# Two attention layers over patches: who reads layer 1's logits back, and when a patch's reads, jobs and first rows are issued

## The chip, the cores and the metric

The kernel runs on one core of one Trainium2 chip. TensorE (PE in the profile) multiplies matrices, VectorE (DVE), ScalarE (ACT) and GpSimd (POOL) do elementwise work, and SyncE (SP) only issues transfers (DMAs). ScalarE and GpSimd issue DMAs too. Each issuing engine has its own DMA queue: the profile calls SyncE's q1, GpSimd's q0 and ScalarE's q10. Every engine takes its instructions in order, and an instruction that waits holds up all behind it on that engine.

The metric is device time in microseconds, as the median of several runs. Before the change it is 3497.4 us (three runs, 3495.59 to 3503.78).

## What is computed

The input is x, 8 images of 56 x 56 pixels with 384 channels, all in float32. Both layers normalise x in 32 groups of channels, apply an attention over each pixel's 3 x 3 neighbourhood, and add the result to x:

```
layer 0 (12 heads): v = xn Wv;  a = softmax(xn Wa / sqrt(32)), 9 x 9 weights per pixel and head
                    out[p] = sum_q a[p,q] v[neighbour q];  y = out folded back onto the neighbours;  x += y Wo
layer 1 (6 heads):  v = xn W_v + b_v;  a = softmax(xn W_attn + b_attn), 9 weights per pixel and head
                    y = sum_k a[k] v[neighbour k];  x += y W_proj + b_proj
```

## The kernel before

**Tiling.** Two images make a pair (NPAIR = 4), and a pair's column of 2 x 56 = 112 pixels is the unit of work. Layer 0 walks over the 4 x 56 columns, one column a *step*; the step number divided by 56 gives pair and column c. Of eight columns only seven are worked on by themselves: a TensorE tile has 128 rows, so the eighth column's pixels (c % 8 == 7) ride along in the 16 spare rows of the other seven, and that step has no attention of its own. Seven columns make a *patch* (PX = 7, eight patches a pair).

**Layer 0, one step.** `attend` does three logit matmul groups (tile `bank`, from `wa_t`), with VectorE taking maximum and difference of each, ScalarE the exponential, and one matmul group for v. Between these groups `between(n)`, n = 0 to 3, slips in the work of earlier columns: for n = 0 the transposes of the next pair's rows (`turned`, `stats_chunk`, tile `pt` from `xr`), the normalising of the column before (`normalise`, then `presum` on GpSimd, tile `pre`) and one job; for n = 1 the matmul `pw` of `fold` (the column three back); for n = 2 another job; for n = 3 the rest, and one more job in a step with c % 8 == 7. `fold` ends in two writes of the column's weights to the table `ztab` in DRAM, and `keep_v` stores v to `vtab` through GpSimd. `share_out` moves the eighth column's pieces over the scratch tensor `last` or directly (`at`).

**Layer 0, one patch.** When a patch's columns are all in the tables, `fetch_v` (line 765) reads v of both images (vp, 1536 KB each) and one step later `fetch` (line 782) reads the weights of both (z, 2352 KB each; one z tile per image, two vp tiles). `fetch` also queues the patch's ten jobs, all due four steps later: four `contract` jobs (tile `pc`, copied to `yT`) and six `project_out` jobs (tile `po`, added to `xres` as `x1t`). `Jobs.run(step, n)` runs the first n jobs whose due step has come, in the order in which they were queued, so ten jobs run two a step in five steps. `held_back` (line 929) keeps jobs out of two steps near the end.

**Before and around the steps.** At the start (lines 512 to 525) the rows of pair 0 are loaded in 14 blocks, transposed, and copied to DRAM by `keep_block`; then `clear_first` writes zeros into the tables. The rows of the next pair are loaded block by block with `stats_load`, one every three steps, from `upkeep` (line 866), the first one at c = 0, and used three steps later. `upkeep` also clears z at step 8 (lines 874 to 876) and issues the clearing of further tables, six writes each, at steps that `clears` gives. All of these loads, copies, clears, table writes and patch reads are issued by SyncE, in program order.

**Layer 1** works on groups of seven columns (g, 32 of them, m = 0 to 6 within a group), from 2246 us on. `attend` makes logits (tile `lgt`) and v together. When a group is done its logits are written to DRAM by ScalarE (`keep_logits`, table `lgtab`), read back with one pixel row a partition by `read_logits` (line 1073, tile `at`), and then go through `weigh` (maximum and exponential), `share` (sum, reciprocal, product) and `move` (a shift matmul `pw` on TensorE, copies into `wz`, a write to `ztab1`). A group later `fetch` (line 1133) reads z and vp for its contraction:

```
            done, last = g - 1, g == NG
            read, first, second, moved = (0, 2, 3, 4) if last else (1, 3, 4, 5)
...
            if m == 1 and g + 1 < NG:
                load(g + 1)
            if g > 1 and m == 0:
...
                fetch(done - 1, base + step + 3)
            if g and m == read:
                read_logits(done)
```

`weigh` runs at m = 3, `share` at 4, `move` at 5. In layer 1 SyncE's calls are held in program order (`sync` is `InOrder`, line 134 of the profile is its helper); the v stores and the output stores go through `nc.gpsimd` directly, and are placed by the builder.

Of the kernel before, what the change touches and what calls it, by code (L numbers as in the profile page):

```python
# [8 lines left out]
F32 = mybir.dt.float32  # L9
# [6 lines left out]
def two_outlook_layers(  # L16
# [77 lines left out]
    EP1, FIRST1 = 11, 4  # L94
    SLOT0, SLOT1 = EP0 * ROW0, EP1 * ROW1
    LINE0, LINE1 = SX0 * SLOT0 + ROW0, SX1 * SLOT1 + ROW1
    NTAB = 2

    xf = x.rearrange("b y x c -> (b y) x c")
    of = out.rearrange("b y x c -> (b y) x c")  # L100
# [5 lines left out]


    vtab0 = dram.tile([NPX * (R + GAP) + GAP, SX0, C], F32, name="vtab0")
    ztab0 = [dram.tile([RT + 1, LINE0], F32, name=f"ztab0_{n}") for n in range(NTAB)]
    vtab1 = dram.tile([NPX * (R + GAP) + GAP, SX1, C], F32, name="vtab1")  # L110
    ztab1 = [dram.tile([RT + 1, LINE1], F32, name=f"ztab1_{n}") for n in range(NTAB)]
    lgtab = dram.tile([NPAIR * W * R, NA1], F32, name="lgtab")
    xTs = [dram.tile([P, NCH, W * R], F32, name=f"xT_{pair}") for pair in range(NPAIR)]
    x1s = [dram.tile([NPX, P, NCH, T], F32, name=f"x1_{pair}") for pair in range(NPAIR)]
# [306 lines left out]
    def layer0(late, pools):  # L421
# [93 lines left out]
        for blk in range(NBLK):  # L515
# [4 lines left out]
                    pass  # L520
            if blk == 1:
                wv_t = weight(fixed, wv0, C, "wv0_t", sync)
        for blk in (1, 4, 0, 2, 3, *range(5, NBLK)):
            keep_block(0, blk)
        clear_first()
        warm = stat.tile([P, 1], F32, tag="warm", name="warm", bufs=1)
# [195 lines left out]
        def fold(pair, c):  # L722

            pre = pres.pop((pair, c)).rearrange("r (pi qi) f h -> r pi qi f h", qi=K)
            parts = []
            for px, sx in patches_of(c, 2):
                wt, to, f0, f1 = weights_of(sx)
                for e, pi, qi in ((0, 0, 2), (E0 - 1, 2, 0)):  # L730
                    scalar.activation(
                        to[:, e], pre[:, pi, qi, f0:f1, :], AF.Copy, scale=inside[:R, 0, qi : qi + 1]
                    )
                parts.append((px, sx, wt, to, f0, f1))
            pw = ps.tile([R, E0, E0, HEADS0], F32, tag="f", name=f"pw_{pair}_{c}")
            for qi in (0, 2):
                lo = qi // 2
                matmul(
                    pw[:, 2 - qi + lo : 4 - qi + lo], shift[:, qi, :], pre[:, lo : lo + 2, qi],
                    start=(qi == 0), stop=(qi == 2), skip_group_check=True,  # L740
                )
            for px, sx, wt, to, f0, f1 in parts:
                vector.tensor_tensor(
                    to[:, 1 : 1 + K], pw[:, 1 : 1 + K, f0:f1, :], pre[:, :, 1, f0:f1, :], ALU.add
                )
            yield
            for px, sx, wt, to, f0, f1 in parts:
                at = sx * SLOT0 + FIRST0 * ROW0
                table = ztab0[(pair * NPX + px) % NTAB]
                first = table.offset + MARGIN * LINE0 + at  # L750
                weights = wt.rearrange("r e h m -> r e (h m)")
                sync.dma_start(
                    bass.AP(table.tensor, first + ROW0, [[LINE0, R], [1, K * ROW0]]),
                    weights[:, 1 : 1 + K].rearrange("r e a -> r (e a)"),
                )
                sync.dma_start(
                    bass.AP(
                        table.tensor, first + LINE0,
                        [[LINE0, R], [(E0 - 1) * ROW0 - 2 * LINE0, 2], [1, ROW0]],
                    ),  # L760
                    weights[:, 0 : E0 : E0 - 1],
                )
            yield

        def fetch_v(pair, px):

            vps[:] = [patch_tiles(f"0_{pair}_{px}", b) for b in range(IMG)]
            for b in range(IMG):
                rows_to_patches(sync, vps[b], vtab0, px, b * H, PY0, NPY0, SX0)

        vps = []

        xres = {}

# [4 lines left out]
                lambda: sync.dma_start(xres[pair, px], xTs[pair][:, :, px * T : (px + 1) * T])  # L779
            )  # L780

        def fetch(pair, px, due, final=None):

            nm = f"0_{pair}_{px}"
            n_tile = 2
            yT = projected(nm)
            if not pair and not px:
                load_res(0, 0)
            for b in range(IMG):
                z, vp = zs[b], vps[b]  # L790
                bands(
                    sync, z, ztab0[(pair * NPX + px) % NTAB], LINE0, SLOT0, ROW0, 0, GROUPS0,
                    b, PY0, NPY0,
                )

                def contract(t, b=b, z=z, vp=vp):
                    pc = ps.tile([P, NCH, n_tile, PY0, PX], F32, tag="c", name=f"pc_{nm}_{b}_{t}", bufs=NC)
                    for n in range(n_tile):
                        py = t * n_tile + n
                        zp = z[: SX0 * SY0, py].rearrange("s (y h m) -> s y h m", y=PY0, h=HEADS0)  # L800
                        for h in range(HEADS0):
                            i, j = divmod(h, P // D0)
                            matmul(
                                pc[j * D0 : (j + 1) * D0, i, n],
                                vp[: SX0 * SY0, py, h * D0 : (h + 1) * D0],
                                zp[:, :, h, :],
                                start=True, stop=True,
                            )
                    rows_of = slice(t * n_tile * PY0, (t + 1) * n_tile * PY0)
                    scalar.copy(  # L810
                        yT[:, :, :, b, rows_of], pc.rearrange("p i n y m -> p i m (n y)")
                    )

                for t in range(0, NPY0 // n_tile, NC):
                    jobs.add(due, lambda t=t, f=contract: [f(t + n) for n in range(NC)])
            if pair == NPAIR - 1 and px == NPX - 1:
                jobs.add(due, clear_bands)
            if px == 0:
                st1s[pair] = stat.tile([P, NCH, IMG, 2 * NPX, 6], F32, tag="st1", name=f"st1_{pair}")

            def project_out(half, j):
# [2 lines left out]
                po = ps.tile([P, 4 * R], F32, tag="o", name=f"po_{nm}_{half}_{j}")  # L824
                project_half(po, wo_t, yT, half, j)
                if j == 0:
                    fetch.x1t = late_w.tile([P, NCH, 4, R], F32, tag="x1t", name=f"x1t_{nm}_{half}", bufs=2)
                x1t = fetch.x1t
                vector.tensor_tensor(
                    x1t[:, j].rearrange("p m r -> p (m r)")[:, :n], po[:, :n],  # L830
                    xres[pair, px][:, j, lo * R : hi * R], ALU.add,
# [16 lines left out]
                        if following[0] < NPAIR:  # L848
                            load_res(*following)

            for half in range(2):
                for j in range(NCH):
                    jobs.add(due if final is None else final, lambda half=half, j=j: project_out(half, j))
            if px == NPX - 1:
                def params_part(n):
                    if n == 0:
                        making["1"] = norm_params(st1s.pop(pair), f"1_{pair}", params1, pair)
                    next(making["1"])

                for n in range(3):  # L860
                    jobs.add(due, lambda n=n: params_part(n))

        making = {}
        clearing = list(clears())
# [1 line left out]
        def upkeep(step):  # L866

            pair, c = divmod(step, W)
            if pair == 0:
                if c == 1:  # L870
                    gpsimd.memset(wts, 0.0)
                if c == 3:
                    sync.dma_start(wo_t, wo0.rearrange("(i p) n -> p i n", p=P))
                if c == 8:
                    for z in zs:
                        nc.gpsimd.memset(z, 0.0)
            while clearing and clearing[0][0] <= step:
                clearing.pop(0)[1]()
            if pair + 1 < NPAIR:
                blk, i = divmod(c - 3, NCH)  # L880
                if 0 <= c and i == 0 and blk < NBLK - 1:
                    stats_load(pair + 1, blk + 1, sync, xr_tile(pair + 1, blk + 1))
                if NBLK * NCH + 3 <= c < NBLK * NCH + 6:
                    if c == NBLK * NCH + 3:
# [24 lines left out]
        for step in range(NPAIR * W + LAG):  # L909
# [16 lines left out]
                if normal:  # L926
                    keep_v(*divmod(step - 1, W))

            held_back = NPAIR * W - 4 < step < NPAIR * W - 1

            def between(n):

                if n == 0:
                    next(turning, None)
                    weigh()
                    jobs.run(step, 0 if held_back else 1)
                elif n == 1:
                    next(folding, None)
                    next(turning, None)
                elif n == 2:  # L940
                    jobs.run(step, 0 if held_back else 1)
                else:
                    for part in summing:
                        next(part)
                    next(folding, None)
                    if step % SB == NTILE:
                        jobs.run(step, 1)
# [6 lines left out]
                    between(n)  # L954
            flush()

            pair, c = divmod(step - LAG - PX, W)
            if pair >= 0 and c % PX == 0:
                fetch_v(pair, c // PX)
            pair, c = divmod(step - LAG - PX - 1, W)  # L960
            if pair >= 0 and c % PX == 0:
                fetch(pair, c // PX, step + 4)

        def last(due):
            fetch_v(NPAIR - 1, NPX - 1)
            fetch(NPAIR - 1, NPX - 1, due, due + PX + 2)

        return step + 1, last, late_w

# [8 lines left out]
    def layer1(pools, base, last_of_layer0, late_w):  # L978
# [94 lines left out]
        def read_logits(g):  # L1073

            lgs[g] = work.tile([R, PX, K2, HEADS1], F32, tag="at", name=f"at_1_{g}")
            sync.dma_start(
                lgs[g].rearrange("r m k h -> r m (k h)"),
                bass.AP(
                    lgtab.tensor, lgtab.offset + g * T * NA1, [[NA1, R], [R * NA1, PX], [1, NA1]]
# [23 lines left out]
        def move(g):  # L1103
# [14 lines left out]
            for kj in range(K):  # L1118
                dst = wz[:, kj * K * ROW1 : kj * K * ROW1 + PX * step].rearrange("r (m e) -> r m e", e=step)
                dst = dst[:, :, : K * ROW1].rearrange("r m (e h o) -> r e m h o", e=K, h=HEADS1)  # L1120
                for e in range(K):
                    scalar.copy(dst[:, e, :, :, 0], pw[:, e, :, kj, :])
            table = ztab1[g % NTAB]
            scalar.dma_start(
                bass.AP(
                    table.tensor, table.offset + MARGIN * LINE1 + FIRST1 * ROW1,
# [5 lines left out]
        def fetch(g, due):  # L1132
# [4 lines left out]
            vps = [patch_tiles(f"1_{g}", b)[: SX1 * SY1, :NPY1] for b in range(IMG)]  # L1137
            for b in range(IMG):
                bands(
                    sync, zs1[(g * IMG + b) % NZ], ztab1[g % NTAB], LINE1, SLOT1, ROW1, MARGIN - 1,  # L1140
                    GROUPS1, b, PY1, NPY1,
                )
            for b in range(IMG):
# [155 lines left out]
```

## Time and profile before

| | |
|---|---|
| median of three runs | 3497.4 us |
| profiled execution | 3500.61 us |
| its span in the profile | 3498.6 us |
| first step's matmuls start | 60.05 us |
| TensorE busy, 200 to 2200 us (layer 0) | 90.7 to 98.9 of each 100 us |
| TensorE busy, 2200 to 2400 us | 78.8 and 90.9 of 100 us |
| TensorE busy, 2400 to 3400 us (layer 1) | 94.8 to 98.3 of each 100 us |
| SyncE's queue q1 | 678.54 MB, 61.4% of the 16 DMA engines' time |
| GpSimd's queue q0 | 148.12 MB, 13.3% |
| ScalarE's queue q10 | 23.40 MB, 2.8% |

Times are from the start of the span. "Idle before" is the time in which an engine stood still ahead of an instruction, with the instruction or DMA that ended it behind the arrow. "Waits" sums these by releaser. L134 is a helper line through which many operations are recorded, so the tile names tell which one it is. PEclk is the TensorE clock that was granted, in tenths of full speed. A stall costs time only where the stalled engine is the one that everything else ends up waiting for.

### The profile page before, as it was taken

The numbers are of one execution on the slowest core, as the hardware profiler recorded it, in microseconds if no ns is written. First come the engines' busy times: TensorE is split into PE (matmuls) and PEld (weight loads), VectorE is DVE, ScalarE is ACT, GpSimd is POOL, SyncE is SP. The second block draws the span as 40 slices with busy tenths as digits, with TensorE's granted clock in tenths as the row PEclk, the third lists the DMA queues.
The fourth block names the chain that finished last, engine by engine and source line by source line (L and its number), as shares of the span: only waits on it lengthen the run. The fifth ranks groups of instructions, "written<-read, shape, count | busy, mean of one in ns | idle before, by whom it ended". The sixth has DMA issues, their size and how long they took to land. (4 is left out here: it accounts for less than half of the span.)

```text
span 3498.6 us, 74335 instructions
## 1 busy us (share of the span) xinstructions
PE 3245.2 (93%) x28510; PEld 2193.7 (63%) x28510; DVE 1866.6 (53%) x4786; ACT 1354.1 (39%) x3749; POOL 1367.7 (39%) x1982
## 2 busy tenths in 40 slices
PE   6789999999999899999988999889999999999997
PEld 5567666667666666766666666445555555555565
DVE  5567776667677667767665677333223222222231
ACT  3334434444444344444333343223333434324332
POOL 3545454545455544555554555322212212212220
PEclk8899999999999999999999999899999999999998
DMA  9689797779878878987786777966787777777775
GB/s 289 183 294 308 259 301 264 235 253 322 294 241 286 272 237 264 308 292 236 241 271 218 256 261 238 337 173 194 213 224 197 213 213 201 213 209 200 221 198 145
DMA packets 592893, 854.81 MB, mean 244 GB/s; under 512 B 205602, under 2 KB 468090, under 8 KB 588442
## 3 DMA queue, kind: packets, MB, share of 16 engines
q1 hardware_dynamic: 473946, 678.54, 61.4%
q0 software_dynamic: 59136, 148.12, 13.3%
q10 hardware_dynamic: 59456, 23.40, 2.8%
q8 instruction: 224, 3.67, 0.5%
q14 instruction: 131, 1.07, 0.1%
HBM read 520.28 MB, written 326.07 MB: 242 GB/s over the span
## 5 line engine op out<-in xcount | busy, mean ns | idle before, releaser
L119 PE MATMUL bank<-wa_t,xn 128*128 128x288 f32 x3528 | 979.0, 416 | 4.2 <-ACT xn L134 2.1
L119 PE MATMUL po<-yT,wo_t 128*128 128x448 f32 (+1 forms) x2304 | 829.4, 502 | 28.2 <-DVE x1t L134 22.6
L134 POOL TENSOR_TENSOR at<-at,den 128x972 f32<-128x972 f32 x196 | 440.5, 2247 | 932.7 <-DVE den L134 533.2
L119 PEld LDWEIGHTS bank<-wa_t,xn 128*128 128x128 f32 x3528 | 655.7, 193 | 219.5 <-issue 21.1
L119 PEld LDWEIGHTS po<-yT,wo_t 128*128 128x128 f32 x2304 | 432.5, 193 | 331.8 <-issue 200.7
L134 ACT ACTIVATE at<-at 128x972 f32<-128x972 f32 (+1 forms) x228 | 215.3, 944 | 1086.1 <-DVE at L134 1082.6
L332 POOL DMA_DIRECT2D vtab<-v x392 | 212.9, 546 | 861.8 <-DVE v L134 801.2
L119 PE MATMUL bank<-wc_t,xn 128*128 128x438 f32 x1176 | 488.5, 553 | 0.0
L134 DVE TENSOR_REDUCE mx<-bank 128x36 f32<-128x324 f32 x588 | 284.7, 484 | 349.1 <-PE bank L119 345.6
L119 PEld LDWEIGHTS pc<-z,vp 121*32 121x32 f32 (+1 forms) x17664 | 341.3, 121 | 153.4 <-issue 118.0
L119 PE MATMUL bank<-wv_t,xn 128*128 128x384 f32 x1176 | 425.5, 499 | 3.6 <-DVE at L134 3.6
L119 PE MATMUL pc<-z,vp 121*32 121x49 f32 (+1 forms) x17664 | 380.5, 220 | 31.3 <-issue 23.5
L134 DVE TENSOR_TENSOR at<-bank,mx 128x324 f32<-128x324 f32 x588 | 291.2, 495 | 154.7 <-ACT pre L134 55.7
L119 PEld LDWEIGHTS bank<-wc_t,xn 128*128 128x128 f32 x1176 | 220.1, 198 | 163.7 <-issue 158.2
L119 PEld LDWEIGHTS bank<-wv_t,xn 128*128 128x128 f32 x1176 | 223.5, 193 | 141.6 <-issue 17.2
L134 ACT COPY yT<-pc 128x294 f32<-128x294 f32 (+2 forms) x512 | 192.6, 403 | 285.4 <-PE pc L119 282.9
L134 POOL DMA_DIRECT2D vtab<-v x476 | 289.4, 612 | 10.7 <-issue 5.3
L134 DVE TENSOR_TENSOR lgt<-bank,ba_t 128x54 f32<-128x54 f32 x196 | 41.6, 212 | 446.4 <-PE bank L119 446.4
L134 POOL TENSOR_TENSOR pre<-at,at 112x108 f32<-112x108 f32 (+1 forms) x440 | 224.2, 527 | 78.2 <-DMA at<-last 41.6
L134 ACT ACTIVATE xn<-xin,bias,scale 128x168 f32<-128x168 f32 (+1 forms) x474 | 208.5, 504 | 0.0
L134 ACT ACTIVATE wts<-pre,inside 112x48 f32<-112x48 f32 (+4 forms) x672 | 181.2, 358 | 70.4 <-DMA ztab<-wts 38.9
L134 ACT COPY ot<-pt 112x384 f32<-112x384 f32 x128 | 61.4, 480 | 355.9 <-PE pt L122 342.2
(115 smaller groups left out, 2987.8 us busy)
## 6 DMA issues: line engine op xcount, KB each, us to landing
z<-ztab SPq DMA_DIRECT2D x64, 2352.0 KB
vp<-vtab SPq DMA_DIRECT2D x64, 1536.0 KB
vp<-vtab SPq DMA_DIRECT2D x64, 945.0 KB
xres<-xT SPq DMA_DIRECT2D x32, 1176.0 KB
ztab<-wts SPq DMA_DIRECT2D x336, 110.2 KB
vtab<-v POOLq DMA_DIRECT2D x108, 336.0 KB, 6.4
xin<-xT SPq DMA_DIRECT2D x52, 672.0 KB
xr<-in_x SPq DMA_DIRECT2D x50, 672.0 KB
```

The costliest lines, as they stand in the source:

```text
L119: tc.keep_in_program_order(nc.tensor.matmul(*args, **kwargs))
L134: return lambda *args, **kwargs: tc.keep_in_program_order(op(*args, **kwargs))
L332: queue.dma_start(bass.AP(table.tensor, table.offset + first, [*([line * step, count] for step, count in rows_of or ((1, rows),)), *([[(R ...
```

## The change

Seven edits:

- `read_logits` is issued by `nc.gpsimd` in place of SyncE, and no longer held in program order.
- In layer 0 a patch's four reads go out one a step, in the order v of image 0, z of image 0, v of image 1, z of image 1. They begin in the step in which both v reads went out before.
- The jobs get due steps of their own: counted from the step of the first z read, the contractions in steps 3, 4, 5 and 5 (before: from 4 on), the projections in 6, 6, 7, 8, 8 and 9. The sixth patch of the last pair gets its projections one a step from 6 to 11, and `last`, the last patch's, has due steps that match. `held_back` goes.
- The first rows of pair 1 are asked for at the start, behind the copies of four blocks, and not at c = 0 of the steps.
- The clearing of both z tiles at step 8 goes.
- Layer 0 keeps two tables for its weights; layer 1 gets three in place of two, so one more is cleared, at step 194.
- `assert` and bookkeeping (`waiting`, `vps` as a dictionary) have no instructions on the chip.

```diff
-    NTAB = 2
+    NTAB0, NTAB1 = 2, 3
...
-        for blk in (1, 4, 0, 2, 3, *range(5, NBLK)):
+        for blk in (1, 4, 0, 2):
+            keep_block(0, blk)
+        stats_load(1, 0, sync, xr_tile(1, 0))
+        for blk in (3, *range(5, NBLK)):
             keep_block(0, blk)
...
-        def fetch_v(pair, px):
-            vps[:] = [patch_tiles(f"0_{pair}_{px}", b) for b in range(IMG)]
-            for b in range(IMG):
-                rows_to_patches(sync, vps[b], vtab0, px, b * H, PY0, NPY0, SX0)
+        def fetch_v(pair, px, b):
+            vps[pair, px, b] = patch_tiles(f"0_{pair}_{px}", b)
+            rows_to_patches(sync, vps[pair, px, b], vtab0, px, b * H, PY0, NPY0, SX0)
+        def fetch_z(pair, px, b):
+            bands(
+                sync, zs[b], ztab0[(pair * NPX + px) % NTAB0], LINE0, SLOT0, ROW0, 0, GROUPS0,
+                b, PY0, NPY0,
+            )
...
-                for t in range(0, NPY0 // n_tile, NC):
-                    jobs.add(due, lambda t=t, f=contract: [f(t + n) for n in range(NC)])
+                for due, t in zip((first, second)[b], range(0, NPY0 // n_tile, NC)):
+                    waiting.append((pair, px, b))
+                    jobs.add(due, lambda t=t, b=b, f=contract: contracts(t, b, f))
...
-            for half in range(2):
-                for j in range(NCH):
-                    jobs.add(due if final is None else final, lambda half=half, j=j: project_out(half, j))
+            parts = [(half, j) for half in range(2) for j in range(NCH)]
+            for due, part in zip(last, parts):
+                jobs.add(due, lambda part=part: project_out(*part))
...
-                if c == 8:
-                    for z in zs:
-                        nc.gpsimd.memset(z, 0.0)
...
-                if 0 <= c and i == 0 and blk < NBLK - 1:
+                if i == 0 and blk < NBLK - 1 and pair + c:
...
-            held_back = NPAIR * W - 4 < step < NPAIR * W - 1
...
-                    jobs.run(step, 0 if held_back else 1)
+                    jobs.run(step, 1)
...
-            pair, c = divmod(step - LAG - PX, W)
-            if pair >= 0 and c % PX == 0:
-                fetch_v(pair, c // PX)
-            pair, c = divmod(step - LAG - PX - 1, W)
-            if pair >= 0 and c % PX == 0:
-                fetch(pair, c // PX, step + 4)
+            for lag, read, b in ((0, fetch_v, 0), (1, fetch_z, 0), (2, fetch_v, 1), (3, fetch_z, 1)):
+                pair, c = divmod(step - LAG - PX - lag, W)
+                if pair >= 0 and c % PX == 0 and c // PX < NPX:
+                    px = c // PX
+                    read(pair, px, b)
+                    if lag == 1:
+                        ends = [step + n for n in (6, 6, 7, 8, 8, 9)]
+                        if pair == NPAIR - 1 and px == NPX - 3:
+                            ends = [step + n for n in range(6, 12)]
+                        plan(pair, px, (step + 3, step + 4), (step + 5, step + 5), ends)
...
-            fetch_v(NPAIR - 1, NPX - 1)
-            fetch(NPAIR - 1, NPX - 1, due, due + PX + 2)
+            for b in range(IMG):
+                fetch_v(NPAIR - 1, NPX - 1, b)
+                fetch_z(NPAIR - 1, NPX - 1, b)
+            plan(
+                NPAIR - 1, NPX - 1, [due] * 2, [due + 2] * 2, [due + PX + 2 + n // 2 for n in range(6)]
+            )
...
-            sync.dma_start(
+            nc.gpsimd.dma_start(
                 lgs[g].rearrange("r m k h -> r m (k h)"),
...
-            table = ztab1[g % NTAB]
+            table = ztab1[g % NTAB1]
```

## The prediction

> **What bounds the kernel now.** I read the page's busy shares and slices first. TensorE is busy for 93% of the span and no other engine for more than 53%, so the time is TensorE's work, its idle time (3498.6 - 3245.2 = 253.4 us) and what it loses to a clock below full speed.
>
> ```profile
> PE 3245.2 (93%) x28510; PEld 2193.7 (63%) x28510; DVE 1866.6 (53%) x4786; ACT 1354.1 (39%) x3749; POOL 1367.7 (39%) x1982
> PE   6789999999999899999988999889999999999997
> PEclk8899999999999999999999999899999999999998
> ```
>
> The slices put the idle time at the start, at the change of layers (slice 26), and thinly elsewhere. The waits of TensorE name the releasers (us in total, times, longest):
>
> ```profile
> PE pw L119 <- POOL pre L134: 42.8, 15, 6.3
> PE pw L119 <- DVE at L134: 35.1, 22, 4.9
> PE pt L122 <- DMA xr<-in_x: 30.7, 6, 11.2
> PE po L119 <- DVE x1t L134: 22.6, 31, 2.2
> ```
>
> The timeline places them. In layer 0 the long ones come early (start, duration, what, idle time before it and its releaser):
>
> ```profile
> 94.59 0.98 PE L122 MATMUL pt<-ident,xr 112*128 112x112 f32 x4 [11.21 <-DMA xr<-in_x]
> 141.46 1.14 PE L119 MATMUL pw<-pre,shift 112*112 112x120 f32 x4 [6.25 <-POOL pre L134]
> 142.40 3.10 PE L119 MATMUL bank<-wa_t,xn 128*128 128x288 f32 x6
> 205.17 0.98 PE L122 MATMUL pt<-ident,xr 112*128 112x112 f32 x4 [10.82 <-DMA xr<-in_x]
> ```
>
> The reader is to see the second loss: the six matmuls after the 6.25 us stall took 3.10 us where such a group normally takes 1.63 (row at 149.66). So a stall costs itself plus a slow stretch: +1.9 us after 94.59, +2.6 after 141.46, +2.5 after 205.17 (each row's duration less that of the same group later).
>
> In layer 1 (from 2246 us) each group of seven columns repeats one chain, here at 3050 us: logits written, read back, VectorE's maximum, and TensorE's shift matmul.
>
> ```profile
> 3050.49 9.37 DMA lgtab<-lgt
> 3059.88 13.50 DMA at<-lgtab
> 3073.40 0.83 DVE L134 TENSOR_REDUCE mx<-at 112x42 f32<-112x378 f32 x1 [9.06 <-DMA at<-lgtab]
> 3078.18 1.32 PE L119 MATMUL pw<-at,shift 112*112 112x126 f32 x6 [1.85 <-DVE at L134]
> ```
>
> From all 30 groups after 2347 us: the write takes 9.1 to 15.8 us; the read 2.5 to 13.5, mean 5.5; groups whose maximum starts within 18 us of the write's issue stall TensorE by at most 0.2, later ones by up to 3.6. Their stalls before the shift matmul (its own wait and the one on ACT ot just before) sum to 39.9 us without the last group, and eight of them leave the matmul at 1.3 to 1.6 us for 0.82, with the next group slow too (3.04 to 3.69 for 2.37), about 2 us each: 16 us.
>
> **The change, part by part** (gain positive; bounds in brackets).
>
> 1. *First rows of pair 1* move from behind all 14 xT copies and the clears (issued at 84.85 in SyncE's timeline) to behind four (about 44 us). One DMA moves, past ten copies, which wait some 2 us more for 672 KB at the 283 to 377 GB/s of these stretches; nothing reads these until blocks are loaded again. The stall at 94.59 is worth 11.21 + 1.9 = 13.1. Next is the second block's rows: behind six table clears (101.19 to 109.9), already 2.37 late at 120.52, and TensorE now comes sooner. I take **+10** [5, 13].
>
> 2. *The two z memsets go.* Both are 4.04 us on GpSimd. The one at 134.94 stands just ahead of the pre that TensorE awaits at 141.46, so 6.25 becomes about 2.2; less slow clock makes it **+5** [0, 8.9]. The one at 77.14 must be gone too for part 1: it stood ahead of the pre of column 0.
>
> 3. *One read a step.* The four reads per patch (vp 2 x 1536 KB, z 2 x 2352 KB) were issued in two steps, 7.8 MB together; every later SyncE DMA queues behind them. At 185.92 both z reads go out, at 193.25 the rows of the next block, which TensorE awaits until 205.17. With only 2352 KB ahead these rows save 2352 KB of queue at near 380 GB/s (fortieths of 60 to 210 us show 344 to 409 when full), 6 us, and SyncE's waits on ztab writes (5.4 us there) shrink. The stall is worth 10.82 + 2.5; the first contraction, a step earlier, will wait some 3 for its z: **+10** [3, 13]. The same pattern returns each pair (1.60 at 403.04, 2.87 at 948.89, 1.84 at 1495.01, 546 us or 56 steps of 9.75 apart): **+6** [0, 8]. Waits of VectorE on last<-at that reach TensorE (0.68, 1.44, 2.90): half, **+2.5** [0, 5].
>
> 4. *The reads' lateness.* Image 0's contraction moves from four steps after its z read to three, image 1's has three from a later issue. In SyncE's and TensorE's timelines the first pc mostly starts 18 to 26 us after the z issue, but 11 to 12.7 in a patch of each pair, where the issue falls in a step without attention (454.15 to 466.71, no stall). One step less leaves 5 to 7 us there; a 2352 KB read needs 6 us at 380 GB/s plus the 2.5 us of a quiet read: 2 late. With the short steps around image 1's reads I take **-6** [-40, 0]; -40 is three patches a pair late by 3.3 (12.5, the longest a first z read can have taken there, less some 9). WAR on z and ztab0 (two tables) loses two steps of four: ztab writes of patch px+2 come two steps after the last z read is issued, 18 us against some 9, so I charge nothing; uncovered it would be inside the -40.
>
> 5. *The jobs.* A patch's ten jobs ran two a step in five steps of seven; now 1, 1, 2, 2, 1, 2, 1. In steps with c % 8 = 7 TensorE has only jobs and waits on GpSimd: with no job it lost 2.51 + 2.53 (662.86, 670.99) and 0.98 + 3.71 (586.38, 593.74), two such passes a pair; with two jobs nothing. A contraction is 1.45 us, a projection 1.86 to 2.27. Now no pass is empty, but four of seven have one job a step: about 2.4 us left at each, as much as before, 9.7 a pair: **0** [-10, 10]. Fewer projections back to back: waits on x1t in layer 0 are 17.5 us, I take **+5** [0, 10]. Without held_back and with the sixth patch's projections one a step, the three crowded ones at 2207 to 2217 (2.22 + 0.60 + 0.60, and 0.92 and 2.75 on pre) thin out: **+3** [-3, 7].
>
> 6. *Third ztab1.* The write of group g's weights meets reads of two groups before, issued a whole group (37 us) ahead, so the wait it removes is already nil. It adds six clears on SyncE at step 194. Six fills took 8.73 us at 101.19; after the set due at step 186, z came 21.4 us behind vp for 13 to 17 elsewhere, and stalls of 0.76, 2.90 and 2.20 followed; after the set of step 178 none stand out: **-3** [-6, 0].
>
> 7. *Logits read by GpSimd.* Same 165 KB, 32 times, about 0.55 us of issue each on an engine busy 20%. It waits for the logits' write at the head of GpSimd's queue: behind it stand the v stores and out stores. SyncE's waits for lgtab sum to 365.6 us in 31, 12 each: two v stores delayed by up to two steps, with five v buffers, and patches are read a group later; nothing waits. What counts is the landing. On SyncE's queue it is behind z, vp and x1t (4.1 MB, all issued within 10 us). GpSimd's rows: 2 to 4 us for v stores when quiet (3074 to 3087), 7.2 to 9.1 in the burst (3052 to 3062), where its queue took 34% against 62%, and 60 against 44 at 3060 to 3062. So a lower end of 2.5 clears all stalls, 39.9 + 16 and 2 to 5 of the tail, +58; an upper end of 9, 3.5 above SyncE's mean, costs 30 groups x 3.5 and slow clock, -125. By the state at the time of issue, mostly the burst's end, I take 5 after a late write and 6.5 after an early one: the early writes (9.4, 12.3, 12.9, 13.5) lose their 8 to 13.5 us reads, which is 15 us of stalls and 5 of clock; the six reads of 2.5 to 2.9 get slower, 10 back: **+10** [-125, 58].
>
> The Trainium skill speaks against this part. "DMA: Bandwidth & Descriptors", Rules for kernel authors, says that spreading transfers over the issuing engines does not help, since they share the 16 DMA engines; Specifications gives a first byte after about 1 us on GpSimd's path and 0.6 on SyncE's. By that alone 32 reads would land 0.4 later, an estimate of 13 us lost, and by it the sum would end at 3478. The trace shows the other side: a read of 13.5 us on SyncE's queue that had only 165 KB of its own.
>
> **Sum:** 10 + 5 + 10 + 6 + 2.5 - 6 + 0 + 5 + 3 - 3 + 10 = 42.5 us. The profiled execution took 3500.61 (2.0 beyond its span), so 3458; it lies 3.2 over the median 3497.4, hence **3455**.
>
> **Rivals.**
> *Full relief:* GpSimd's read always lands in about 2.5 us. For: its quiet rows, and its share at 3060. Against: the write takes 15 us because the DMA engines are full. Part 7 gives 58 for 10: 3407.
> *Lateness:* the spread reads miss their contractions (part 4 at -40). For: 12.5 us patches; SyncE runs up to 14 us behind TensorE at 186. Against: the queue ahead is halved. 3455 + 34 = 3489.
> *GpSimd's read is later than SyncE's.* Place: the maximum in each layer 1 group. Each us above 5.5 costs 30 us; the rest of the change gains 32.5, so it decides from 6.6 us. At 7.8, between its quiet and burst rows: 69 lost, 3455 + 10 + 69 = 3534, slower. For: 7 to 9 us in the burst, 784 pieces of 216 bytes, and its v and out stores ahead in the same queue. Against: most writes land at the burst's end.
> *It does not do what it says:* the GpSimd call is not held in program order, so the read may be placed later among the v stores; priced with the rival before.
>
> **Numbers.** Forecast case (3425 to 3480) 0.46; full relief 0.22; lateness 0.15; GpSimd's read later 0.17. The range runs from full relief with a little more out of parts 1 to 3, 3390, to the slower rival, 3535. Measurement tells 0.3% (10.5 us) from no change: faster is 0.46 + 0.22 + 0.06 of lateness = 0.74; same 0.08 of lateness + 0.01; slower 0.16 + 0.01.
>
> **What would show it.** No xr wait near 90 and 200; no z memset at 135 and a pre wait under 3; pc waiting on z (part 4, wrong if over 1 us in most patches); pw waiting on pre unchanged in sum; at<-lgtab landing (part 7) and layer 1's pw waits under 30 us. If layer 0 keeps its length to 2210 us, parts 1 to 3 are wrong; if layer 1 is longer, part 7 is.

## The result: 57 us slower, and the profile after

The changed kernel takes **3557.5 us** (median of four runs, 3548.3 to 3562.3); the kernel before, beside it, 3500.3. The ratio is 1.016, with a 95% interval of 1.014 to 1.019. The forecast was 3455: the sign is wrong, and the time lies 22 us above the range. The profiled execution took 3548.31 us, with a span of 3546.6.

From here on times of different sets of runs are compared by their ratios to the kernel before in the same set (its median was 3493 to 3500 us); one per cent is 35 us.

The page after, the same rows as those shown of before:

```profile
PE 3244.9 (91%) x28510; PEld 2212.9 (62%) x28510; DVE 1869.9 (53%) x4786; ACT 1354.6 (38%) x3749; POOL 1389.4 (39%) x2012
PE   7889999999999889999989899789999999999997
PEclk8999999999999999999999999899999999999999
```

TensorE's busy time did not change (3245.2 before). All of the 48 us by which the span grew are idle time: 301.7 us in place of 253.4. The first two slices are fuller than before; of the later ones up to the change of layers, the 15th, 23rd and 26th are emptier and one is fuller. TensorE's waits after (us in total, times, longest) name the cause:

```profile
PE pc L119 <- issue: 74.9, 20, 10.5
PE pc L119 <- DMA z<-ztab: 66.0, 19, 9.2
PE pw L119 <- DVE at L134: 33.7, 22, 5.2
PE pw L119 <- POOL pre L134: 15.8, 12, 4.1
PE po L119 <- DVE x1t L134: 14.5, 15, 1.9
...
PE pt L122 <- DMA xr<-in_x: 6.0, 1, 6.0
```

Three rows fell as meant: pre 42.8 to 15.8, x1t 22.6 to 14.5, xr 30.7 to 6.0. The contraction (pc) rose to the top. All its stalls in the trace sum to 158 us in layer 0, against 31 before; 44 single ones are over 1 us. Of the 74.9 us with "issue" as the releaser, 58.4 stand at the start of a contraction, like those put down to z; the other 16.6 fall between the matmuls of one contraction. TensorE's timeline of one contraction of image 1 (start, duration, what, idle time before it and its releaser):

```profile
1237.95 1.62 PE L119 MATMUL bank<-wa_t,xn 128*128 128x288 f32 x6
1239.41 0.55 PE L122 MATMUL pt<-ident,xr 112*128 112x112 f32 x4
1248.21 2.19 PE L119 MATMUL pc<-z,vp 121*32 121x49 f32 x96 [8.25 <-DMA z<-ztab]
1250.32 3.16 PE L119 MATMUL bank<-wa_t,xn 128*128 128x288 f32 x6
```

TensorE stands for 8.25 us until z has landed, and then works slowly: six logit matmuls take 3.16 us in place of 1.62. SyncE's timeline shows what was issued ahead of that z:

```profile
1223.50 0.44 SPq L134 DMA_DIRECT2D xr<-in_x  x1
1227.32 0.58 SPq L134 DMA_DIRECT2D xin<-xT  x1
...
1228.92 0.55 SPq L134 DMA_DIRECT2D x<-x1t  x1
1229.52 0.64 SPq L134 DMA_DIRECT2D xres<-xT  x1
1230.20 1.40 SPq L134 DMA_DIRECT2D z<-ztab  x1
```

Image 1's z is asked for at 1230.20 and its contraction can start at 1248.21: **18.0 us**. Just ahead of it in the same queue stand xres (1176 KB), the x1t store, xin and xr (672 KB each), and the DMA engines have no room in that time (stretch, its length, busy times by engine, granted clock, DMA share, GB/s):

```profile
1236.00:1242.00 6.00, 3.96 (x17) 2.56 (x15) 3.39 (x9) 3.20 (x7) 1.30 (x3) 1.00 1.04 370
1242.00:1248.00 6.00, 0.00 (x0) 0.00 (x0) 1.39 (x4) 0.00 (x0) 4.37 (x6) 0.59 1.01 367
1248.00:1254.00 6.00, 5.79 (x108) 4.81 (x109) 0.48 (x1) 1.68 (x6) 0.98 (x2) 0.56 0.47 141
```

The reader is to see a full queue (share 1.0, 370 GB/s) that empties just as TensorE is let go, and a clock that has been cut meanwhile. The reader is to compare the other reads, over the first 30 patches. Where an image's first contraction waited, image 1's z landed 15.7 to 20.1 us after its issue (18.4 at 592.89, 17.9 at 2014.47) and image 0's 9.1 to 14.7 (12.5 at 574.70). Without its stall, image 1's first contraction would have come 6.5 to 20.5 us after the issue, 14.5 in the median. The stalls are 120 us for image 1 and 31 for image 0.

Where the time was lost is read by the start of the k-th matmul pw of layer 0 in both traces: the first is 11.4 us earlier than before, the 29th 4.8 earlier, the 57th 1.6 later, the 113th 17 later, the 197th 51 later, and layer 1's first logits are written 61 us later. So the start gained, and the patches after it lost that and more. Layer 1 gave some 11 us back (its last logits are 51 later).

Layer 1's chain did not change its length. The reads of its logits by GpSimd, in a busy and in a quiet moment (two groups of the timeline after):

```profile
2887.13 0.88 POOL L1092 DMA_DIRECT2D at<-lgtab  x1
2899.48 0.83 DVE L134 TENSOR_REDUCE mx<-at 112x42 f32<-112x378 f32 x1 [6.07 <-DMA at<-lgtab]
...
3087.78 0.92 POOL L1092 DMA_DIRECT2D at<-lgtab  x1 [10.65 <-PE bank L119]
3091.07 0.84 DVE L134 TENSOR_REDUCE mx<-at 112x42 f32<-112x378 f32 x1 [5.38 <-DMA at<-lgtab]
```

From issue to the maximum it is 12.3 us and 3.3 us. From the logits' write to the maximum it is 18.8 us in the mean over all 32 groups, 19.2 before; the wait of the shift matmul on VectorE sums to 33.7 us, 35.1 before.

### The profile page after: what moved, and what is told of

Its sections match the earlier page's. It is cut to its first block, busy times and chain, and to the rows that moved or that the text cites. A ratio compares the mean times of both kernels' runs of the same rounds, so it can differ in the third digit from the quotient of the medians.

```text
span 3546.6 us, 74270 instructions
## 1 busy us (share of the span) xinstructions
PE 3244.9 (91%) x28510; PEld 2212.9 (62%) x28510; DVE 1869.9 (53%) x4786; ACT 1354.6 (38%) x3749; POOL 1389.4 (39%) x2012
## 3 DMA queue, kind: packets, MB, share of 16 engines
q14 instruction: 131, 1.07, 0.1%
## 5 line engine op out<-in xcount | busy, mean ns | idle before, releaser
L119 PE MATMUL bank<-wa_t,xn 128*128 128x288 f32 x3528 | 1002.3, 422 | 2.8 <-ACT xn L134 2.1
L119 PE MATMUL po<-yT,wo_t 128*128 128x448 f32 (+1 forms) x2304 | 819.9, 497 | 25.4 <-DVE x1t L134 14.5
L119 PEld LDWEIGHTS bank<-wa_t,xn 128*128 128x128 f32 x3528 | 667.8, 197 | 223.8 <-issue 23.2
L119 PE MATMUL pc<-z,vp 121*32 121x49 f32 (+1 forms) x17664 | 388.8, 225 | 158.2 <-issue 74.9
L119 PEld LDWEIGHTS pc<-z,vp 121*32 121x32 f32 (+1 forms) x17664 | 351.1, 125 | 272.6 <-issue 204.3
L119 PE MATMUL bank<-wv_t,xn 128*128 128x384 f32 x1176 | 415.9, 490 | 0.0
```

The costliest lines, as they stand in the source:

```text
L119: tc.keep_in_program_order(nc.tensor.matmul(*args, **kwargs))
```

## The experiments

Three theories stood at first. A: contractions wait for z, which lands later than they are due. B: the jobs, spread thin, leave TensorE idle in other places. C: reads spread over four steps get slower, with the rest of SyncE's queue.

**Every job a step later** (the last three patches of all excepted, here and below):

```diff
-    ends = [step + n for n in (6, 6, 7, 8, 8, 9)]
+    off = 0 if pair == NPAIR - 1 and px > NPX - 4 else 1
+    ends = [step + off + n for n in (6, 6, 7, 8, 8, 9)]
...
-    plan(pair, px, (step + 3, step + 4), (step + 5, step + 5), ends)
+    plan(pair, px, (step + off + 3, step + off + 4), (step + off + 5, step + off + 5), ends)
```

> The changed kernel with every job of layer 0 due one step later (contractions 4, 5, 6, 6 steps after the first z read, projections 7, 7, 8, 9, 9, 10), the last three patches as they were. Theory A, the contractions come before their z has landed: TensorE's waits before pc fall from 158 us to under 50 and the time from 3557 to about 3450. Theory B, the thin jobs (one a step in four steps of seven) lose the time: the spread is as thin as before, so the time stays within 15 us of 3557. Theory C, SyncE's queue as such is slower when the reads are spread: stays within 15 us as well, with the waits moved to other tiles.

Measured: **3395.1 us**, ratio 0.972 [0.970, 0.974]: 155 us better than the change (1.016), and 98 better than before, below the 3450 expected. Its page and TensorE's waits ahead of pc:

```profile
PE 3215.4 (95%) x28510; PEld 2191.7 (64%) x28510; DVE 1863.3 (55%) x4786; ACT 1350.2 (40%) x3749; POOL 1390.4 (41%) x2012
...
PE pc L119 <- issue: 5.7, 3, 3.1
...
PE pc L119 <- ACT yT L134: 5.3, 4, 1.5
```

The stalls of pc fall from 158 to 11 us, and TensorE is busy 29.5 us less with the same matmuls, at a higher mean granted clock (0.969, against 0.954 after). Theory A holds: no first contraction of the first 30 patches waits any more, with 13.7 us or more between the issue of image 0's z and its contraction and 17.9 or more for image 1. The other edits together are worth 98 us when their jobs are not late, over twice what I had forecast for them.

**Only image 1's contractions, and the projections, a step later:**

```diff
-    plan(pair, px, (step + 3, step + 4), (step + 5, step + 5), ends)
+    plan(pair, px, (step + 3, step + 4), (step + off + 5, step + off + 5), ends)
```

> The changed kernel with only image 1's contractions (and the projections) a step later; image 0's stay three and four steps after their z read. Lateness: in the changed kernel's trace the first image's first contractions waited some 50 us and the second's some 100 of the 158 us. So pc waits of about 50 us remain and the time lies two thirds of the way from 3557 to 3395, near 3450. If image 0 is what counts, it stays above 3500.

Measured: 3427.5 us, 0.981 [0.977, 0.986]; pc's stalls 26 us, where about 50 and 3450 were expected. So some 120 of the 155 us hang on image 1, whose z is issued two steps after image 0's (the projections, which moved with it, are in this figure), and 33 on image 0.

**The reads paired as before, the new jobs kept:**

```diff
-    for lag, read, b in ((0, fetch_v, 0), (1, fetch_z, 0), (2, fetch_v, 1), (3, fetch_z, 1)):
+    for lag, read, b in ((0, fetch_v, 0), (0, fetch_v, 1), (1, fetch_z, 0), (1, fetch_z, 1)):
...
-    if lag == 1:
+    if lag == 1 and b == 0:
```

> The changed kernel with the reads issued as before the change (both v in one step, both z in the next), and the new jobs. Theory A: image 1's z goes out two steps sooner, so its contractions no longer wait; image 0's still do, by more, since two z reads share the queue. pc waits 60 to 100 us, time 3490 to 3520. Theory B: within 15 us of 3557 or above. Theory C: the time falls to that of the kernel before or below, about 3480, with the xr waits back.

Measured: 3471.1 us, 0.994 [0.992, 0.995]; pc's stalls 73 us. Image 1's z, two steps earlier, takes half of the lateness away, as A has it: image 1's contractions stall for 11 us in place of 120, image 0's for 58 in place of 31. It was quicker than I had expected, since I still priced the rest of the change too low.

**Image 1's z ahead of its step's traffic, the changed kernel's due steps kept:**

```diff
-    for lag, read, b in (..., (2, fetch_v, 1), (3, fetch_z, 1)):
+    for lag, read, b in (..., (2, fetch_v, 1)):
...
+    pair, c = divmod(step - LAG - PX - 3, W)
+    if pair >= 0 and c % PX == 0 and c // PX < NPX:
+        fetch_z(pair, c // PX, 1)
     if step < NPAIR * W:
         attend(*divmod(step, W), between)
```

> The changed kernel with one edit: the read of z for image 1 is issued ahead of its step's attention, loads and stores in place of behind them; the jobs keep the changed kernel's due steps. It tells how much of the 18 us from issue to landing is place in SyncE's queue. Theory A (z lands late because xr, xin, x1t and xres, some 3 MB, stand ahead of it in the same queue): image 1's z lands 12 us or less after its issue, the stalls of pc in layer 0 fall from 158 us to 50 to 80, and the time from 3557 to 3440 to 3480. Rival (the 16 DMA engines are full in these stretches, whatever the order): the 3 MB of the step then go beside z, it lands as late as before, pc's stalls stay over 120 and the time over 3520.

Measured: 3437.4 us, 0.982 [0.980, 0.984]; pc's stalls 63 us. SyncE's timeline for the patch shown above:

```profile
1227.62 0.77 SPq L134 DMA_DIRECT2D vp<-vtab  x1
1228.44 5.38 SPq L134 DMA_DIRECT2D z<-ztab  x1
...
1242.80 2.26 SPq L134 DMA_DIRECT2D xres<-xT  x1
```

z now follows 0.8 us behind v (16.4 after) and xres stands behind it; image 1's contraction, 30.8 us after the issue, no longer waits for it here. No byte was taken away, and 120 us came back: the stalls are those that theory A named, 50 to 80 us. But that z also lands sooner after its issue, in 12 us or less, as A had it, is not shown. In the four of the first 30 patches where image 1's first contraction still waited, z took 17.7 to 23.7 us, no less than in the changed kernel; in the others it is only known to have landed by the contraction, 17.6 us or more after the issue. What grew is the time to be had, from 14.5 us to 24.9 in the median. So the experiment shows that an earlier issue removes the stalls. Whether z takes so long because of what stands ahead of it in its own queue, or because the DMA engines are full in whatever order, it leaves open. Of the stalls left, some 22 us are waits for image 0's z and 12 for image 1's; the rest are small ones between contractions of one step.

**The late jobs, but two a step**, to ask what the thin schedule is worth:

```diff
-    ends = [step + off + n for n in (6, 6, 7, 8, 8, 9)]
+    ends = [step + off + n for n in ((6, 6, 7, 7, 8, 8) if off else (6, 6, 7, 8, 8, 9))]
...
-    (step + off + 3, step + off + 4)
+    (step + 4 * off + 3 * (1 - off) + off, step + off + 4)
```

> The version with later jobs, with the jobs lumped two a step again (contractions 5, 5, 6, 6, projections 7, 7, 8, 8, 9, 9 steps after the first z read; last three patches unchanged). Two of seven steps have no job again. If thin jobs are worth nothing, as the prediction had it, 3395 within 10 us. If the thin jobs are what makes this version 100 us faster than the kernel before, it falls back to 3430 or more, with the waits of pw on GpSimd's pre and slow clock back.

Measured: 3451.8 us, 0.988 [0.983, 0.992]: 55 us worse than the thin schedule (0.972; one job in four steps of seven, two in three). Theory B has the wrong sign: thin jobs gain. TensorE is busy for 3245.8 us against 3215.4 (3222.3 and 3225.7 in two versions below with the same jobs), so 20 to 30 of the 55 are matmuls that take longer. The rest is idle time, most of it in the rows below: two contractions in one step share two pc tiles and their copies to yT. The waits of pw on pre, which were expected back, are not (27.0 us against 31.5).

```profile
PE pw L119 <- issue: 17.6, 13, 2.6
...
PE pc L119 <- ACT yT L134: 16.3, 11, 2.1
```

In the thin schedule these rows are 7.9 and 5.3.

**The kernel before with thin, later jobs and nothing else** (the jobs that make layer 1's parameters move with them):

```diff
+    at = due + (0, 1, 2, 2)[2 * b + n] if thin else due
-    jobs.add(due, lambda t=t, f=contract: [f(t + n) for n in range(NC)])
+    jobs.add(at, lambda t=t, f=contract: [f(t + n) for n in range(NC)])
...
+    at = due + (3, 3, 4, 5, 5, 6)[NCH * half + j] if thin else due if final is None else final
-    jobs.add(due if final is None else final, lambda half=half, j=j: project_out(half, j))
+    jobs.add(at, lambda half=half, j=j: project_out(half, j))
```

> The kernel before with the jobs alone changed: contractions 4, 5, 6 and 6 steps after the z reads, projections 7, 7, 8, 9, 9 and 10 (the last three patches of all as before); reads two a step, first rows, z clears and SyncE's logits read as before. Theory A (thin jobs are worth some 50 us by themselves, as the run with two jobs a step stood 57 us above the one with thin jobs): 3430 to 3455, TensorE busy some 20 to 30 us less. Rival (thin jobs gain only with the spread reads): 3470 or more.

Measured: **3423.7 us**, 0.978 [0.975, 0.980]: 78 us gained by the due steps alone, more than the 45 to 70 expected. The spans differ by 70.7 us, of which 20.3 are busy time and 50.4 idle. TensorE's timeline of a place where the kernel before stalled twice (583 to 595 us), first before, then here:

```profile
586.38 0.64 PE L119 MATMUL pw<-pre,shift 112*112 112x120 f32 x4 [0.98 <-issue]
586.85 3.18 PE L119 MATMUL bank<-wa_t,xn 128*128 128x288 f32 x12
593.74 1.14 PE L119 MATMUL pw<-pre,shift 112*112 112x120 f32 x4 [3.71 <-POOL pre L134]
```

```profile
575.99 1.86 PE L119 MATMUL po<-yT,wo_t 128*128 128x336 f32 x6
578.02 0.64 PE L119 MATMUL pw<-pre,shift 112*112 112x120 f32 x4 [0.17 <-issue]
580.57 3.60 PE L119 MATMUL po<-yT,wo_t 128*128 128x336 f32 x6 [1.92 <-DVE x1t L134]
...
585.47 1.86 PE L119 MATMUL po<-yT,wo_t 128*128 128x336 f32 x6
...
588.62 0.58 PE L119 MATMUL pw<-pre,shift 112*112 112x120 f32 x4
```

Projections stand ahead of both pw, and the wait on pre is gone; one of them waits 1.92 us for x1t itself. Over layer 0 from 150 us on (stalls of at least 0.6 us), pw's stalls ahead of pre fall from 41.9 to 24.7 us, pc's from 27.6 to 11.2.

**The start alone, on the kernel before:** first rows behind four copies, no clearing of z.

> The kernel before with two edits: the first rows of pair 1 are asked for behind four copies, and z is not cleared at step 8. The prediction's parts 1 and 2 said 15 us together: 3485. If the start's stalls only move to the next rows and the first patch, the time stays within 5 us of 3500.

Measured: 3482.3 us, 0.997 [0.995, 0.998]: 11 us gained. pre falls from 42.8 to 32.3, pt on xr from 30.7 to 22.4.

**Every job a step later, the reads paired** (the first and the third diff above together), to price the spread reads:

> The changed kernel with all jobs a step later and the reads paired as before the change. It tells what the spread itself is worth once nothing is late. If the spread relieves the rows behind the reads: 10 to 20 us slower than the spread one (3395), so 3405 to 3415, with waits on xr near the first patch back. If the spread is worth nothing and the jobs are all: 3390 to 3400. If spread reads are a loss that the later jobs only cover: faster than 3390.

Measured: 3415.9 us, 0.976 [0.972, 0.981], against 0.972 [0.970, 0.974] with the reads spread. The middle of the difference is 15 us; the intervals overlap a little. pt waits 17.2 us on xr, against 6.6. C has the wrong sign: the spread reads, once the jobs wait for them, are no loss and probably a gain. Thin and later jobs (78 us), the start (11) and the spread (15) sum to 104 us, and the version with all of them gains 98, so little is left for the other edits.

**The GpSimd read alone, on the kernel before**, one word of the diff (`sync` to `nc.gpsimd` in `read_logits`):

> The kernel before with one edit: layer 1's logits are read back by GpSimd. By the spans of layer 1 in the two traces (the last group's logits are written 61 us later in the changed kernel at the start of the layer and 51 us later at its end, and the tail gains 3 more) this edit alone gives 10 to 15 us: about 3487. If the gain there comes from the third table or from what layer 0 hands over, the time stays within 4 us of 3500. If GpSimd's read is the loss, it is slower than 3510.

Measured: 3497.3 us, 1.001 [0.999, 1.003]: no change. The wait of pw on VectorE is 38.6 us, 35.1 before.

**The late jobs with SyncE reading the logits:**

> The version with later jobs, its logits read by SyncE as before the change. The one-edit kernel gave 1.001 [0.9991, 1.0028] for GpSimd's read, so within 8 us of 3395. If GpSimd's read is worth the 13 us by which layer 1 was shorter in the changed kernel's trace, 3408.

Measured: 3406.6 us, 0.975 [0.972, 0.979], against 0.972 with GpSimd. The middle of the difference is 11 us in favour of GpSimd, a little over the 8 us named, but the intervals overlap, so none is shown.

**The late jobs with two tables in layer 1** (`NTAB0, NTAB1 = 2, 2`):

> The changed kernel with its layer 0 jobs a step later (3395 us before), and layer 1 with two weight tables in place of three, so that six clears of SyncE at step 194 go. Theory: the third table costs 3 us (0 to 6) and removes no wait, so 3389 to 3398, not told from no change. Rival: it removes waits of ztab1's writes on reads two groups before, and layer 1 gets over 10 us longer.

Measured: 3402.6 us, 0.971 [0.969, 0.973], the same as with three (0.972); the time itself lies above the 3389 to 3398 named, as the kernel before does in this set by 5 us. The third table costs nothing that shows, and serves nothing that shows.

**The late jobs with image 1's z ahead** (the first and the fourth diff together):

> The changed kernel with its layer 0 jobs a step later, and the read of z for image 1 ahead of its step's attention, loads and stores. Only 11 us of pc stalls are left there, so with the theory (contractions wait for z and nothing else of the order matters) at most 5 to 10 us are gained: 3385 to 3398. Rival (z ahead of xr and xres makes those late instead): the waits of pt on xr grow by over 5 us and the time is 3405 or more.

Measured: 3409.0 us, 0.974 [0.971, 0.976]. Above the 3385 to 3398 hoped for, but the interval meets that of the late jobs alone, and the waits of pt on xr grew by 2.2 us only. Neither theory is borne out; once the jobs are late enough, there is nothing left for the order of the reads to give.

## Why the prediction was wrong, point by point

| step of the prediction | forecast, us | measured, us | by |
|---|---|---|---|
| 1, 2: first rows, z clears | +15 | +11 | the start alone |
| 3: one read a step | +18.5 | about +15 (0 is not excluded) | late jobs, spread against paired |
| **4: lateness** | **-6 [-40, 0]** | **-155** | change against late jobs |
| **5: thin jobs** | **+8** | **about +55** | late jobs, thin against two a step |
| 6: third table | -3 | 0 | two tables |
| 7: logits by GpSimd | +10 [-125, 58] | -3 [-10, 3]; +11 (0 is not excluded) | on the kernel before; with late jobs |

- **The step that failed is part 4, in the time that a z read takes to land.** The mechanism was named and was even a rival of its own, with the right sign against the change, but its size was wrong by a factor of 25, and its far end by 4. I wrote that "a 2352 KB read needs 6 us at 380 GB/s plus the 2.5 us of a quiet read", 8.5 us together. Where a contraction waited, image 0's z took 9.1 to 14.7 us and image 1's 15.7 to 20.1. For the patch that I had in mind, one of each pair, this was near: image 0's z took 9.1 to 10.8 us there and was 1.1 to 1.5 late, where I had said 2. For image 1 it was half of what was needed. In the patch shown, some 3 MB of other transfers stood ahead of it in the queue and the DMA engines were full; which of the two makes the read long was not told apart. I had said of other loads in part 3 that "every later SyncE DMA queues behind them", and did not ask it of z itself. Nor were there three full steps of 9.75 us to have it in: z is asked for behind the other transfers of its step, and from there TensorE came to the two contractions shown here in 9.8 and 10.0 us (1239.96 against 1230.20, and 584.71 against 574.70; each start less its stall). A contraction stall of over 1 us stands in 28 of the first 30 patches, not in one a pair; by the prediction's own sign ("wrong if over 1 us in most patches") part 4 was wrong.
- **Image 1 was priced in half a sentence.** "With the short steps around image 1's reads" covered most of it, 120 of the stalls' 152 us in the first 30 patches: its z goes out two steps later while its contractions stay at step 5. The bound of -40 counted "three patches a pair late by 3.3", once each; the trace has 44 stalls over 1 us, up to 10.5.
- **Stalls cost busy time too.** Between the profiled executions of the change and of the late jobs 147 us of pc stalls go, 32 us of other idle time come back (pw's wait on pre alone grows from 15.8 to 31.5), and 29.5 us of busy time go: 144.8 us of span together. The bound of part 4 left the busy time out, although the reading of before had shown it (1.63 to 3.10 us after 6.25).
- **What the kernel before showed.** Its pc waited 0.8 us on z and 23.5 us, in 20 stalls, on "issue". Those 20 all stand directly behind matmuls of a contraction, 17 us or more after the issue of its z, so they are no late reads: before the change z was in time. That was the slack of a step, and not a quick read: image 0's first contraction came 11 to 26 us after the issue.
- **Part 5 was cancelled out by a guess.** "About 2.4 us left at each" of four passes with one job, "as much as before", gave 0. With thin jobs two passes a pair wait, 1.8 to 2.5 us in most, and the contractions wait less on one another's tiles (5.3 us against 16.3). The slower matmuls, which part 5 did not count, are 20 to 30 us of the 55. Some of the 78 us on the kernel before is the step's delay and not the thinness; these two weren't tried apart there.
- **Parts 1 to 3** are right in kind. The stalls at 94.59 and 205.17 are gone, that at 141.46 is 4.07 us at 132.60 (forecast 2.2: GpSimd still has three v stores and a product of its own ahead), and the second block's rows wait 5.98 us at 115.29, where I had named 2.37 as next in line. "If layer 0 keeps its length, parts 1 to 3 are wrong" was too blunt a test: it became longer through part 4.
- **Part 7.** The read lands much as SyncE's did, 3.1 to 12.3 us from its issue to the maximum (2.5 to 13.5 before; means 5.2 and 5.5), and the rival that made the change slower through it falls (0.999 to 1.003). The rule of the Trainium skill, "DMA: Bandwidth & Descriptors", Rules for kernel authors, that spreading transfers over the issuing engines does not help, agrees with this run. The read of 13.5 us that I set against it fell in a stretch where the 16 DMA engines were full (share 1.01 to 1.07 from 3055 to 3070 us), and GpSimd's transfers run on the same engines.
- **The rivals.** Lateness was the right one, at 0.15, priced at 3489. It needed no failure of the other parts to end at 3557: 98 gained and 155 lost. That the forecast was no further off is luck: the other edits gave 98 us where 48.5 were forecast, and hid part of the loss.

The better version is the one with every job a step later: 3395 us, 0.972 of before.

## What to carry to other kernels

When work that waits for a transfer is moved nearer to it, take the landing time from such transfers in a trace under the same traffic, and not from the bytes of the transfer alone: here 9 to 20 us in place of 8.5. A wait that the trace shows as nearly nothing may be hidden by a step of slack, so do not give slack away before its size is known; trying it one step later and one earlier is one number in the code. Work spread thin over the steps was worth some 55 us here over the same work two jobs a step.

## What was not expected of the hardware

**Short stalls can cut the clock.** After a stall of 2.49 us, until 587.20, the next six logit matmuls took 2.71 us in place of 1.63 (TensorE's timeline after; below it stretches, with the granted clock behind the five engines' busy times):

```profile
587.20 1.92 PE L119 MATMUL pc<-z,vp 121*32 121x49 f32 x96 [2.49 <-DMA z<-ztab]
589.05 2.71 PE L119 MATMUL bank<-wa_t,xn 128*128 128x288 f32 x6
```

```profile
587.20:589.00 1.80, 1.80 (x96) 1.73 (x96) 0.25 (x1) 0.41 (x1) 1.79 (x4) 0.63 1.06 349
...
591.60:594.00 2.40, 2.40 (x13) 1.94 (x12) 1.80 (x5) 0.00 (x0) 0.00 (x0) 1.00 1.09 272
```

Full speed is back 4.4 us after the stall's end. In this trace, from 100 to 2200 us, such a slow group (over 2 us) follows one of 19 stalls of 1 to 2 us, eight of the 12 of 2 to 3.4, and all 17 of over 3.4. The Trainium skill, "TensorE: Matmul & The Clock Gate", What's actually happening, puts the cut to half speed after an idle window of about 3.4 us; here 2.5 us of idle time were enough to be followed by a slow stretch of some 4 us. The same 28510 matmuls were busy for 3215 to 3226 us with the work spread thin and for 3246 with it in lumps.

**GpSimd's and SyncE's reads of 165 KB land alike** under load (5.5 us in the mean on SyncE in the kernel before, 4.9 with GpSimd's read alone; the quickest take 2.5 and 3.1), though GpSimd's shares its queue with the v and output stores.
